# Two-layer attention kernel: loads, rotary products, second norm and first scores of the opening group in another order, and the layer-2 transposes of the chances ahead of the values

## Chip, cores and metric

One Trainium2 chip, one core. The metric is the device time of one execution in microseconds (us); three executions of the kernel before took 964.74, 966.09 and 969.46 us, median 966.09. The profile comes from a further execution. Engines are called as in the profile: PE (matrix), PEld (its weight loads), DVE (vector), ACT (scalar), POOL (GpSimd) and SP, which here only issues DMAs.

## What is computed

`x` is 8 batches of 512 tokens of 256 values, all in f32. Two layers:

```
xn = layernorm(x)
x  = x + causal_attention(xn) + int8_linear(xn)        # 16 heads of 64, rotary q and k, biases
xn = layernorm(x)
comparison = (xn @ left) @ (xn @ right).T / sqrt(256)
x  = x + ((comparison > threshold) * softmax(comparison + bias)) @ xn
       + sigmoid(xr @ Wr.T) * (relu(xk @ Wk.T)**2 @ Wv.T)   # xr, xk: mixes of xn and xn one token before
```

The int8 linear quantises `xn` with one scale for all batches, so the greatest absolute value of every batch is gathered while layer 1 runs (`amax`).

## The kernel before

**Order.** The order of the work is written out by hand, and each engine takes its instructions in that order, one queue per engine. What an instruction waits for stops everything behind it on its engine. DMAs are issued by SP, a few by ACT. The built program hands eight completion counters to the DMAs in turn, and a DMA is not issued before the earlier one on its counter has landed.

**Layer 1** runs over 16 groups `at`, two per batch, each of eight heads (four tiles of two heads). The steps of a group:

- `project_qk(p, which)` (L371): the product `pq` (L382, eight matmuls) for one half of a group's q (`which` 0) or k (1), then ACT evicts it with its bias into `l` (L387), and SP copies `l` into `y` with each pair of 32-row blocks exchanged (L389, four DMAs). `l` and `y` have two buffers for each name.
- `turn_qk` (L392): the rotary step. DVE makes `h = l*cos` and `y = y*sin` (L397), POOL adds them (L400). The result `h` is a head tile for the scores; the DMAs of a later `y` wait for this add when they use its buffer.
- `project_v` (L403) with the store of `va` (L418), and `load_v` (L423), which reads it back in another layout as `vr` (four DMAs, L428).
- `scores(at, run)` (L437): products `sc` (L448) for one of five runs of query blocks. `soften` (L455): DVE adds the mask and finds the maximum (L474), ACT makes the exponentials (L478). `divide` (L484): reciprocal on DVE (L489), scaling on POOL (L494). `turn` (L502): DVE transposes the chances (L514). `weigh` (L519): products `av` (L527) of a whole group; it needs all five runs turned.
- `look_at` and `prepare` (L285, L289): statistics and norm of the next batch's `x` on DVE (L151 to L161), with one small POOL step (L155), and `amax` (L293). `transpose_x` (L297): PE transposes it (L303), ACT copies it to `xnT` (L306), SP stores it (L307). The tile of `x` has one buffer.
- `load_rest` and `load_second` (L266, L133): five loads that ACT issues; `wo` is 1 MB.

All products take PSUM banks from one ring of eight, so a product also waits for the reader of the bank eight allocations before.

**The opening** (L714 to L746) is written out apart: batch 0's norm, projections (0,0) to (3,0), the values, and runs 0 and 1 of group 0. The other three runs of group 0 are in the loop at `at == 0` (L783 to L829), with the transposes of batch 1 between runs 2 and 3. The loads of the second half of the weights (`load_group(which, 2, 2)`, L725) and of batch 1 (L722) are issued inside the opening.

**Layer 2** (L901 to L948) runs over batches: `compare` (L595), `key` (L628), `turn_input` for the next batch (L216), `gate` (L642), `sides_of` (L228), `value` (L656), `turn_chances` (L668: PE transposes `trc`, ACT and DVE copy them in turn), `complete` (int8 part) and `end` (products `po`, L687, and output).

Of the kernel before, what the change touches and what calls it, by code (L numbers as in the profile page):

```python
# [8 lines left out]
F32 = mybir.dt.float32  # L9
# [3 lines left out]
ALU = mybir.AluOpType  # L13
# [31 lines left out]
def two_layers(  # L45
# [30 lines left out]
    def load_x(b, parts=1):  # L76
        t = xpool.tile([P, NT, D], F32, tag="x", name=f"x_{b}")
        for h in range(parts):
            rows = slice(h * NT // parts, (h + 1) * NT // parts)
            nc.sync.dma_start(t[:, rows, :], tokens(b)[:, rows, :])  # L80
        return t
# [4 lines left out]
    def load_group(which, g, n=1):  # L86
        nc.sync.dma_start(wqkv[which][:, g : g + n], (Wq, Wk, Wv)[which][:, g : g + n])
# [160 lines left out]
    with ExitStack() as c0:  # L248
# [37 lines left out]
            xt = x_next.pop(0)  # L286
            seen[b] = xt, statistics(xt, f"a{b}", parts=2 if b == 0 else 1)

        def prepare(b):  # L289
            xt, stats = seen.pop(b)  # L290
            normalise(xt, xt, stats)
            normed[b] = xt
            nc.vector.tensor_reduce(  # L293
                amax[:, b : b + 1], xt, AX.XY, ALU.max, apply_absolute_value=True
            )

        def transpose_x(b):  # L297
            xn = normed.pop(b)
            xnT[b] = whole(f"xnT_{b}")
            for k in range(NK):  # L300
                pb = bank(f"pxt_{b}_{k}")
                for t in range(NT):
                    nc.tensor.transpose(  # L303
                        pb[:, bass.ts(t, P)], xn[:, t, bass.ts(k, P)], ident
                    )
                nc.scalar.copy(xnT[b][:, k, :], pb)  # L306
            nc.sync.dma_start(xn_far[b], xnT[b].rearrange("p k n -> p (k n)"))  # L307


        spread = {}  # L310
# [80 lines left out]

        def turn_qk(at, which):  # L392

            l, y = evicted.pop((at, which))
            h = qk.tile([P, 2, S], F32, tag=f"h{which}", name=f"h_{at}_{which}")
            for dst, src, table in ((h, l, cs[:, :S]), (y, y, cs[:, S : 2 * S])):
                nc.vector.tensor_tensor(  # L397
                    dst, src, table[:, None, :].to_broadcast([P, 2, S]), ALU.mult
                )
            nc.gpsimd.tensor_tensor(h, h, y, ALU.add)  # L400
            heads_of[at, which] = h

        def project_v(at):  # L403
            b, g = divmod(at, NH)
# [309 lines left out]
        look_at(0)  # L714
        prepare(0)
        transpose_x(0)
        project_qk(0, 0)
        project_qk(0, 1)
        turn_qk(0, 0)
        project_qk(1, 0)  # L720
        turn_qk(0, 1)
        x_next.append(load_x(1))  # L722
        project_qk(1, 1)
        for which in (1, 0, 2):
            load_group(which, 2, 2)  # L725
        turn_qk(1, 0)
        project_v(0)
        turn_qk(1, 1)
        look_at(1)
        prepare(1)  # L730
        project_qk(2, 1)
        project_qk(2, 0)
        scores(0, 0)
        soften(0, 0)
        turn_qk(2, 1)
        divide(0, 0)
        project_qk(3, 1)
        load_v(0)
        load_rest()
        load_second()  # L740
        turn_qk(2, 0)
        project_qk(3, 0)
        scores(0, 1)
        soften(0, 1)
        turn(0, 0)
        divide(0, 1)  # L746
        for at in range(last):
            b, g = divmod(at, NH)
            two = at + 2 <= last
            if at >= 1:  # L750
                if g == 0 and b < B - 1:
                    fetch(b)
                if at in (last - 3, last - 2):
                    s_ = at - last + 3
                    fetch_output(s_, output_tile(f"x1e_{s_}"))
                    xnl = fetch_input(s_, work.tile([P, NK, S], F32, tag="xnl", name=f"xnl_{s_}"))
                scores(at, 0)
                turn(at - 1, 4)
                soften(at, 0)
                if at == last - 3:  # L760
                    scale_of_x()
                weigh(at - 1)
                keep_weighed(at - 1)
                turn_qk(2 * at + 2, 1)
                load_v(at)
                divide(at, 0)
                turn_qk(2 * at + 3, 1)
                if at == last - 2:
                    first_norm = norm(0, xpool.tile([P, NT, D], F32, tag="x", name="yn_0"))
                scores(at, 1)  # L770
                soften(at, 1)
                turn(at, 0)
            if g == 1 and b + 2 < B:
                look_at(b + 2)
            if at >= 1:
                divide(at, 1)
                project(at + 1, 0)
            elif at == 0:
                project_v(1)
            if at in (last - 3, last - 2):  # L780
                xq = work.tile([P, NK, S], BF16, tag="xq", name=f"xq_{s_}")
                quantise(s_, xnl, xq)
            if at == 0:  # L783
                turn_qk(3, 1)
            scores(at, 2)
            soften(at, 2)
            if at >= 1:
                turn_qk(2 * at + 2, 0)
            turn(at, 1)
            divide(at, 2)  # L790
            if g == 1 and b + 2 < B:
                prepare(b + 2)
            if at == last - 1:
                turn_qk(2 * at + 3, 0)
            if at >= 1:
                project_v(at + 1)
            else:
                transpose_x(1)
                x_next.append(load_x(2))
            if at == last - 1:  # L800
                break
            scores(at, 3)
            soften(at, 3)
            turn_qk(2 * at + 3, 0)
            turn(at, 2)
            divide(at, 3)
            if g == 0 and 1 <= b < B - 1:
                transpose_x(b + 1)
                if b + 2 < B:
                    x_next.append(load_x(b + 2))  # L810
            if at in (last - 3, last - 2):
                for half in range(2):
                    add_quantised(s_, half, xq, line(f"u_{s_}_{half}"))
            if 1 <= at < last - 1:
                finish(at - 1)
            if at == last - 2:
                first_norm()
            scores(at, 4)
            soften(at, 4)
            turn(at, 3)  # L820
            if two:
                project(at + 2, 1)
            divide(at, 4)
            if at == 0:
                spread_rest()
                spread_second()
                fetch(0)
            if g == 0 and b < B - 1:
                add_biases(b)  # L829
            if at == last - 4:  # L830
                greatest()
# [69 lines left out]
        for b in range(B):  # L901
            if b == 0:
                cut(prob, [P, 2, 4 * pitch(1) + 1, Q], "t1", 2)
                cut(prob, [P, 2, 4 * pitch(2) + 1, Q], "t2", 1)
                cut(work, [P, NP, D], "wo", 2)
            if b + 3 < B:
                fetch_late(b + 3)
            if b > 0:
                compare(b)
                kk = key(b)  # L910
            if b + 1 < B:
                turn_input(b + 1, whole(f"yt_{b + 1}", S + 1))
            if b > 0 and b + 2 < B:
                xq = clip_late(b + 2)
            if b == 0:
                pt = turn_chances(b)
            elif b + 1 < B:
                mix_before(b + 1, 1)
                mix_own(b + 1, 1)
            if b > 0:  # L920
                r = gate(b)
            if b + 1 < B:
                sides_of(
                    b + 1, *(attp.tile([P, S], F32, tag="att", name=f"lr_{b + 1}_{n}") for n in range(2))
                )
            if b == 0:
                mix_before(1, 1)
                mix_own(1, 1)
            if b + 1 < B:
                mix_before(b + 1, 0)  # L930
            if b > 0:
                for half in range(2):
                    value(b, half, r, kk)
            if b + 3 < B:
                round_late(b + 3)
            if b > 0:
                pt = turn_chances(b)
            if b + 2 < B:
                complete(b + 2, xq)
            if b + 1 < B:  # L940
                mix_own(b + 1, 0)
            y = work.tile([P, NT, D], F32, tag="v", name=f"y_{b}", bufs=2)
            end(b, (0,), pt, r, y)
            if b + 2 < B:
                normal = norm(b + 2, by_tokens(cuts["t0"][(b + 2) % 3]))
            end(b, (2,), pt, r, y)
            if b + 2 < B:
                normal()  # L948
# [66 lines left out]
```

## Time and profile before

| | |
|---|---|
| profiled execution | 965.37 us; span in the trace 963.6 us |
| busy share of the span | PE 97%, DVE 81%, POOL 58%, ACT 55% |
| mean granted PE clock | 0.993 |
| first score product of group 0 | starts at 42.54 us |
| `weigh` of group 0 | starts at 82.15, ends at 91.75 us |
| last product | ends at 959.95 us |

The page gives busy shares of the engines, the span in 40 slices, the chain of work that ended last, and groups of instructions. A row of a timeline reads: start, duration, engine, line, operation, output from input, count, and in brackets the idle time of the engine before it with what ended it. A row of the waits reads: who waited for what, us in total, times, longest. A row of the windows reads: the stretch and its length, busy us of PE, PEld, DVE, ACT and POOL with instruction counts, the granted PE clock, the DMA share and GB/s.

### The profile page before, as it was taken

The numbers are of one execution on the slowest core, as the hardware profiler recorded it, in microseconds if no ns is written. First come the engines' busy times: TensorE is split into PE (matmuls) and PEld (weight loads), VectorE is DVE, ScalarE is ACT, GpSimd is POOL, SyncE is SP. The second block draws the span as 40 slices with busy tenths as digits, with TensorE's granted clock in tenths as the row PEclk, the third lists the DMA queues.
The fourth block names the chain that finished last, engine by engine and source line by source line (L and its number), as shares of the span: only waits on it lengthen the run. The fifth ranks groups of instructions, "written<-read, shape, count | busy, mean of one in ns | idle before, by whom it ended". The sixth has DMA issues, their size and how long they took to land.

```text
span 963.6 us, 27433 instructions
## 1 busy us (share of the span) xinstructions
PE 935.6 (97%) x10491; PEld 596.7 (62%) x10491; DVE 784.7 (81%) x2429; ACT 529.8 (55%) x1480; POOL 561.3 (58%) x698
## 2 busy tenths in 40 slices
PE   9898999999999999999999998999998999999998
PEld 5345565656565565757565655665655677777776
DVE  4598988797889879978997897787899478888864
ACT  3364565555565656474756655554667335555553
POOL 3396766665655657566666664989766424444321
PEclk9999999999999999999999999999999999999999
DMA  6784345425453544254544435353444112221110
GB/s 183 210 244 103 97 111 153 102 77 139 145 116 83 136 136 128 73 133 116 127 108 133 115 88 155 111 155 89 94 118 123 45 59 71 70 77 55 34 33 33
DMA packets 60930, 105.40 MB, mean 109 GB/s; under 512 B 7552, under 2 KB 38272, under 8 KB 60800
## 3 DMA queue, kind: packets, MB, share of 16 engines
q1 hardware_dynamic: 58928, 102.01, 39.2%
q8 instruction: 83, 1.36, 0.7%
q10 hardware_dynamic: 1872, 1.64, 0.6%
q14 instruction: 47, 0.39, 0.1%
HBM read 39.14 MB, written 28.84 MB: 71 GB/s over the span
## 4 chain that ended last, share of the span: by engine, by line
PE 90%; DVE 4%; issue 2%; POOL 1%; DMA 1%; ACT 1%; SPq 1%; DVEq 0%; ACTq 0%; POOLq 0%
PE pq L382 21%; PE av L527 13%; PE sc L448 13%; PE pw L346 11%; PE pv L411 10%; PE po L687 5%; PE pg L649 3%; PE pvv L661 3%; PE pk L634 3%; PE plr L233 2%; PE trc L674 1%; PE c L606 1%; DVE y L397 1%; DVE p L474 1%; DVE t L514 1%
## 5 line engine op out<-in xcount | busy, mean ns | idle before, releaser
L478 ACT ACTIVATE p<-p,nm 128x64 f32<-128x64 f32 (+15 forms) x512 | 260.0, 511 | 151.6 <-DVE nm L474 122.0
L494 POOL TENSOR_SCALAR p<-p,rs 128x64 f32<-128x64 f32 (+15 forms) x512 | 268.4, 546 | 51.0 <-DVE rs L489 48.7
L400 POOL TENSOR_TENSOR h<-h,y 128x1024 f32<-128x1024 f32 x64 | 167.7, 2621 | 185.4 <-DVE y L397 97.3
L474 DVE CUSTOM_DVE_ANT_0 p<-sc,cmask 128x64 f32<-128x64 f32 (+15 forms) x512 | 191.1, 436 | 80.9 <-PE sc L448 78.9
L514 DVE STREAM_TRANSPOSE t<-p 128x256 f32<-128x256 f32 (+3 forms) x640 | 192.6, 366 | 18.6 <-POOL p L494 18.5
L448 PE MATMUL sc<-h,h 64*32 64x512 f32 (+15 forms) x4096 | 146.0, 397 | 7.6 <-issue 5.9
L527 PE MATMUL av<-t,vr 32*64 32x96 f32 (+15 forms) x4096 | 129.9, 397 | 7.2 <-issue 7.2
L448 PEld LDWEIGHTS sc<-h,h 64*32 64x32 f32 x4096 | 76.5, 106 | 94.6 <-issue 70.5
L527 PEld LDWEIGHTS av<-t,vr 32*64 32x64 f32 x4096 | 122.2, 132 | 14.3 <-issue 10.4
L382 PE MATMUL pq<-xnT,wk 128*128 128x512 f32 x256 | 116.1, 606 | 5.8 <-DMA wk<-in_Wk 4.3
L387 ACT ACTIVATE l<-pq,cs 128x512 f32<-128x512 f32 x128 | 84.3, 682 | 67.6 <-PE pq L382 57.8
L397 DVE TENSOR_TENSOR y<-y,cs 128x1024 f32<-128x1024 f32 x64 | 109.0, 1704 | 8.9 <-DMA y<-l 6.5
L382 PE MATMUL pq<-xnT,wq 128*128 128x512 f32 x256 | 114.4, 598 | 0.2 <-ACT xnT L306 0.2
L346 PE MATMUL pw<-wo,att 128*128 128x256 f32 x512 | 114.3, 381 | 0.0
L411 PE MATMUL pv<-wv,xnT 128*128 128x512 f32 x256 | 114.0, 598 | 0.0
L346 PEld LDWEIGHTS pw<-wo,att 128*128 128x128 f32 x512 | 95.9, 190 | 16.1 <-issue 3.7
L478 ACT ACTIVATION_READ_ACCUMULATOR p<-p,nm 128x1 f32 x512 | 97.0, 189 | 0.0
L382 PEld LDWEIGHTS pq<-xnT,wk 128*128 128x128 f32 x256 | 47.9, 192 | 67.2 <-issue 62.6
L411 PEld LDWEIGHTS pv<-wv,xnT 128*128 128x128 f32 x256 | 47.4, 190 | 57.7 <-issue 54.2
L382 PEld LDWEIGHTS pq<-xnT,wq 128*128 128x128 f32 x256 | 47.4, 190 | 56.6 <-issue 48.1
L397 DVE TENSOR_TENSOR h<-l,cs 128x1024 f32<-128x1024 f32 x64 | 78.4, 1225 | 4.3 <-ACT l L387 4.3
L541 ACT ACTIVATE att<-av,cs 128x512 f32<-128x512 f32 x64 | 38.9, 688 | 72.5 <-PE av L527 72.4
(111 smaller groups left out, 954.8 us busy)
## 6 DMA issues: line engine op xcount, KB each, us to landing
y<-l SPq DMA_DIRECT2D x256, 128.0 KB, 2.3
va<-v SPq DMA_DIRECT2D x32, 512.0 KB, 3.0
vr<-va SPq DMA_DIRECT2D x64, 256.0 KB, 4.6
x<-in_x SPq DMA_DIRECT2D x15, 512.0 KB, 4.2
xnf<-xnT SPq DMA_DIRECT2D x8, 512.0 KB, 3.4
x1f<-x SPq DMA_DIRECT2D x7, 512.0 KB, 3.4
out<-y SPq DMA_DIRECT2D x14, 256.0 KB, 2.2
cut_wo<-xnf SPq DMA_DIRECT2D x5, 512.0 KB, 3.8
```

Source lines behind the costliest of these rows:

```text
L346: nc.tensor.matmul(pw[:, j, :], atts[at, p][:, tok], wo[:, 4 * (at % NH) + p, :], start=(p == 0), stop=(p == 3),)
L382: nc.tensor.matmul(pb, w[:, g, k, bass.ts(t, P)], xnT[b][:, k, :], start=(k == 0), stop=(k == NK - 1),)
L387: nc.scalar.activation(l[:, t, :], pb, AF.Identity, bias=cs[:, bias : bias + 1])
L397: nc.vector.tensor_tensor(dst, src, table[:, None, :].to_broadcast([P, 2, S]), ALU.mult)
L400: nc.gpsimd.tensor_tensor(h, h, y, ALU.add)
L411: nc.tensor.matmul(pb.rearrange("p (g n) -> p g n", g=2), xnT[b][:, k, bass.ts(2 * half + j, P)], wqkv[2][:, 2 * g : 2 * g + 2, k, :], sta ...
L448: nc.tensor.matmul(scored[at, i][e][j * Q : j * Q + Q, :], q[rows, j % 2, bass.ts(i, Q)], k[rows, j % 2, :n], start=True, stop=True,)
L474: nc.vector.tensor_tensor_reduce(p[:, e, col : col + n], sc, cmask[:, S - n :], -1.0 / L**0.5, BIG, ALU.add, ALU.min, nm[:, c : c + 1],)
L478: nc.scalar.activation(p[:, e, col : col + n], p[:, e, col : col + n], AF.Exp, bias=nm[:, c : c + 1], scale=-1.0, accum_out=sm[:, c : c + 1],)
L494: nc.gpsimd.tensor_scalar(p, p, rs[:, c : c + 1], 1.0, ALU.mult, ALU.mult)
L514: nc.vector.transpose(turned[at][c][:, :, at_ : at_ + (n - 1) * pitch(c) + 1 : pitch(c), :], p[:, :, c * P : c * P + n * Q].rearrange("p e ...
L527: nc.tensor.matmul(banks[j][e * L : e * L + L, i * Q :], vs[at][rows, m, c, bass.ts(e, L)], t[c][rows, e, m * pitch(c) + m : m * pitch(c) ...
```

## The change

No product, copy or vector step is added or taken away. The order is changed in two places.

**Opening group.** Batch 1 is loaded straight after batch 0's transposes, and the store of batch 0's transposed input, which stood there, goes behind projection (2,1). The three loads of the second weight half are issued one by one: k behind projection (1,0), q behind (1,1), v behind (2,1). The rotary products are taken apart into `turn_own` (`l*cos`) and `turn_other` (`y*sin` and the add), and the statistics, norm and `amax` of batch 1 stand between them. Runs 0 and 1 of the scores come one after the other, ahead of projections (2,0), (3,1) and (3,0). The loop's special cases for `at == 0` are written out; there, `project_v(1)` comes behind run 2, `turn_qk(3, 0)` ahead of run 3, and the transposes of batch 1 behind the softening of run 3. The spreading of constants, the fetch of batch 0 and its bias add move from the end of group 0 into group 1.

**Layer 2.** For batches after the first, `turn_chances` comes ahead of `value`; for batch 0, the first mix of batch 1 comes ahead of `turn_chances`.

```diff
-        def prepare(b):
+        def prepare(b, *between):
             ...
             normalise(xt, xt, stats)
             normed[b] = xt
+            for f in between:
+                f()
             nc.vector.tensor_reduce(
                 amax[:, b : b + 1], xt, AX.XY, ALU.max, apply_absolute_value=True
             )
+        def keep_input(b):
+            nc.sync.dma_start(xn_far[b], xnT[b].rearrange("p k n -> p (k n)"))
...
+        def turn_own(at, which):
+            h = qk.tile([P, 2, S], F32, tag=f"h{which}", name=f"h_{at}_{which}")
+            times(h, evicted[at, which][0], 0)
+            heads_of[at, which] = h
+        def turn_other(at, which):
+            _, y = evicted.pop((at, which))
+            h = heads_of[at, which]
+            times(y, y, S)
             nc.gpsimd.tensor_tensor(h, h, y, ALU.add)
...
         transpose_x(0)
+        x_next.append(load_x(1))
         project_qk(0, 0)
+        turn_own(0, 0)
+        look_at(1)
+        turn_other(0, 0)
         project_qk(0, 1)
-        turn_qk(0, 0)
+        turn_own(0, 1)
         project_qk(1, 0)
-        turn_qk(0, 1)
-        x_next.append(load_x(1))
+        load_group(1, 2, 2)
+        def second_pair():
+            turn_other(0, 1)
+            turn_own(1, 0)
+        prepare(1, second_pair)
         project_qk(1, 1)
-        for which in (1, 0, 2):
-            load_group(which, 2, 2)
-        turn_qk(1, 0)
+        load_group(0, 2, 2)
+        turn_other(1, 0)
         project_v(0)
         turn_qk(1, 1)
-        look_at(1)
-        prepare(1)
         project_qk(2, 1)
-        project_qk(2, 0)
+        keep_input(0)
+        load_group(2, 2, 2)
         scores(0, 0)
         soften(0, 0)
+        scores(0, 1)
+        project_qk(2, 0)
         turn_qk(2, 1)
         divide(0, 0)
-        project_qk(3, 1)
+        soften(0, 1)
         load_v(0)
         load_rest()
         load_second()
+        project_qk(3, 1)
+        turn(0, 0)
         turn_qk(2, 0)
+        divide(0, 1)
         project_qk(3, 0)
-        scores(0, 1)
-        soften(0, 1)
-        turn(0, 0)
-        divide(0, 1)
+        turn_qk(3, 1)
+        scores(0, 2)
+        soften(0, 2)
+        turn(0, 1)
+        project_v(1)
+        divide(0, 2)
+        turn_qk(3, 0)
+        scores(0, 3)
+        soften(0, 3)
+        transpose_x(1)
+        x_next.append(load_x(2))
+        turn(0, 2)
+        divide(0, 3)
+        scores(0, 4)
+        soften(0, 4)
+        turn(0, 3)
+        project(2, 1)
+        divide(0, 4)
-        for at in range(last):
+        for at in range(1, last):
...
+            if at == 1:
+                spread_rest()
+                spread_second()
+                fetch(0)
+                add_biases(0)
...
+            if b + 1 < B:
+                mix_before(b + 1, 1)
+                mix_own(b + 1, 1)
             if b == 0:
                 pt = turn_chances(b)
-            elif b + 1 < B:
-                mix_before(b + 1, 1)
-                mix_own(b + 1, 1)
-            if b > 0:
+            else:
                 r = gate(b)
             if b + 1 < B:
                 sides_of(
                     ...
                 )
-            if b == 0:
-                mix_before(1, 1)
-                mix_own(1, 1)
+            if b > 0:
+                pt = turn_chances(b)
             if b + 1 < B:
                 mix_before(b + 1, 0)
             if b > 0:
                 for half in range(2):
                     value(b, half, r, kk)
...
-            if b > 0:
-                pt = turn_chances(b)
```

More of the change, by code (lines that the diff above doesn't have):

```diff
@@ L306, in transpose_x @@
                 nc.scalar.copy(xnT[b][:, k, :], pb)
-            nc.sync.dma_start(xn_far[b], xnT[b].rearrange("p k n -> p (k n)"))
+            if b > 0:
+                keep_input(b)
         spread = {}
@@ L392, in turn_qk, with times @@
         def turn_qk(at, which):
-            l, y = evicted.pop((at, which))
-            h = qk.tile([P, 2, S], F32, tag=f"h{which}", name=f"h_{at}_{which}")
[L396 to L399, printed above, removed]
+            turn_own(at, which)
+            turn_other(at, which)
+        def times(dst, src, first):
+            table = cs[:, first : first + S]
+            nc.vector.tensor_tensor(
+                dst, src, table[:, None, :].to_broadcast([P, 2, S]), ALU.mult
+            )
+        def turn_own(at, which):
+            h = qk.tile([P, 2, S], F32, tag=f"h{which}", name=f"h_{at}_{which}")
+            times(h, evicted[at, which][0], 0)
[4 more added lines that the diff above has]
+            times(y, y, S)
             nc.gpsimd.tensor_tensor(h, h, y, ALU.add)
-            heads_of[at, which] = h
         def project_v(at):
@@ L748, in two_layers @@
+        turn(0, 2)
[6 more added lines that the diff above has]
+        for at in range(1, last):
             b, g = divmod(at, NH)
             two = at + 2 <= last
[L750 to L772, printed above, removed]
+            if g == 0 and b < B - 1:
+                fetch(b)
+            if at in (last - 3, last - 2):
+                s_ = at - last + 3
+                fetch_output(s_, output_tile(f"x1e_{s_}"))
+                xnl = fetch_input(s_, work.tile([P, NK, S], F32, tag="xnl", name=f"xnl_{s_}"))
+            scores(at, 0)
+            turn(at - 1, 4)
+            soften(at, 0)
+            if at == last - 3:
+                scale_of_x()
+            weigh(at - 1)
+            keep_weighed(at - 1)
+            turn_qk(2 * at + 2, 1)
+            load_v(at)
+            divide(at, 0)
+            turn_qk(2 * at + 3, 1)
+            if at == last - 2:
+                first_norm = norm(0, xpool.tile([P, NT, D], F32, tag="x", name="yn_0"))
+            scores(at, 1)
+            soften(at, 1)
+            turn(at, 0)
+            if at == 1:
[3 more added lines that the diff above has]
+                add_biases(0)
@@ L773, in two_layers @@
             if g == 1 and b + 2 < B:
                 look_at(b + 2)
[L775 to L779, printed above, removed]
+            divide(at, 1)
+            project(at + 1, 0)
             if at in (last - 3, last - 2):
@@ L782, in two_layers @@
                 quantise(s_, xnl, xq)
-            if at == 0:
-                turn_qk(3, 1)
             scores(at, 2)
             soften(at, 2)
-            if at >= 1:
-                turn_qk(2 * at + 2, 0)
+            turn_qk(2 * at + 2, 0)
             turn(at, 1)
@@ L794, in two_layers @@
                 turn_qk(2 * at + 3, 0)
[L795 to L799, printed above, removed]
+            project_v(at + 1)
             if at == last - 1:
@@ L806, in two_layers @@
             divide(at, 3)
-            if g == 0 and 1 <= b < B - 1:
+            if g == 0 and b < B - 1:
                 transpose_x(b + 1)
@@ L813, in two_layers @@
                     add_quantised(s_, half, xq, line(f"u_{s_}_{half}"))
-            if 1 <= at < last - 1:
-                finish(at - 1)
+            finish(at - 1)
             if at == last - 2:
@@ L823, in two_layers @@
             divide(at, 4)
[L824 to L827, printed above, removed]
             if g == 0 and b < B - 1:
@@ L925, in two_layers @@
                 )
-            if b == 0:
-                mix_before(1, 1)
-                mix_own(1, 1)
+            if b > 0:
+                pt = turn_chances(b)
             if b + 1 < B:
```

## The prediction

> **What bounds the kernel now.** I read the page first. Its span slices show PE busy nearly throughout, so what counts is where PE stands still:
>
> ```profile
> PE   9898999999999999999999998999998999999998
> DVE  4598988797889879978997897787899478888864
> ```
>
> Next the waits of PE over the whole span, to see which of them the change can touch:
>
> ```profile
> PE av L527 <- issue: 7.2, 4, 4.2
> PE sc L448 <- issue: 5.9, 4, 2.5
> PE pq L382 <- DMA wk<-in_Wk: 4.3, 1, 4.3
> PE warm L103 <- POOL ident masks.py:199: 1.8, 1, 1.8
> PE pq L382 <- ACT xnT L306: 1.7, 2, 1.5
> PE pg L649 <- DVE e L622: 1.7, 1, 1.7
> PE sc L448 <- POOL h L400: 1.7, 2, 1.2
> ```
>
> By PE's timeline these fall as follows in the opening: 4.34 us at 29.47 to 33.81 (second weight half of k), 1.50 at 67.45 (`xnT` of batch 1), 0.46 at 76.04, 4.19 ahead of `weigh(0)` at 82.15. The 1.69 us of L649 is at 796.5, in layer 2's batch 1. All other waits lie in untouched stretches. Then the granted clock around the stalls, in the windows (fields: PE, PEld, DVE, ACT, POOL busy, PE clock, DMA share, GB/s):
>
> ```profile
> 34.00:38.00 4.00, 4.00 (x6) 1.60 (x6) 2.83 (x6) 0.69 (x1) 1.71 (x2) 0.57 0.93 326
> 66.00:68.00 2.00, 0.55 (x2) 0.31 (x3) 2.00 (x11) 1.88 (x8) 0.87 (x2) 1.00 0.67 232
> 82.00:86.00 4.00, 3.85 (x42) 3.38 (x50) 4.00 (x15) 2.94 (x9) 0.26 (x1) 0.57 0.67 154
> 594.00:598.00 4.00, 3.34 (x62) 1.60 (x62) 1.31 (x7) 0.58 (x2) 3.81 (x5) 0.57 0.69 157
> ```
>
> After the 4.3 us and 4.2 us stalls the clock is 0.57 for 4 us: the next eight `pq` take 5.37 us for 3.60, so such a stall costs 1.8 us more. The 1.5 us stall (second row) left it at 1.00. The fourth row follows a 2.55 us stall. So all that the change can take away is 4.34+1.77+1.50+0.46+4.19+1.8+1.69 = 15.75 us, 1.6%.
>
> **The opening up to the first scores.** SP issues the k weights at 28.90, behind a transfer that waits for a POOL add, and PE needs them at 29.47. In the new order they stand behind the (1,0) copies, which SP leaves at 24.43; with the old 4.77 us to landing they are there at 29.3. The stall and its slow clock (6.1 us) go. Batch 1's load goes at 8.8, where the store stood; statistics take 2.6 us and fit into DVE's idle 14.3 to 17.4.
>
> What is late next: only projection (2,1) (3.6 us) now stands between the values and `scores(0,0)`, where 8.8 us stood. PE is there at 33.05, and the last head of the pair comes from the add at 32.34 plus 2.34 = 34.7. The norm of batch 1 adds to this: its four L161 steps now fall on POOL's first add (19.7 to 22.1). The nearest row is the norm of another batch beside POOL's L494:
>
> ```profile
> 201.18 0.72 POOL L494 TENSOR_SCALAR p<-p,rs 128x384 f32<-128x384 f32 x1 [0.47 <-DVE rs L489]
> 201.37 0.68 DVE L161 TENSOR_SCALAR x<-x,mv_a,rstd_a 128x256 f32<-128x256 f32 x1
> ```
>
> The norm step ends 0.15 us after POOL's step and took 0.68, where 0.38 to 0.41 is usual with POOL idle. The Trainium skill (SBUF — State Buffer, section Who interferes with whom) says that a DVE instruction with at most one SBUF input and outside the two-port modes does not contend with GpSimd. The norm has one tensor input and costs 0.33 us for 256 elements, the pace per element of the two-input product (1.14 for 1024), so I read it as outside such a mode: by the rule the norm is free and the heads stay at 34.7. By the row it stands until the add ends. Then norm to 23.2, `y` (0,1) to 24.3, `h` (1,0) to 25.4, add to 27.8; the copies of (1,1) wait for that add (26.42 before), and everything behind is 1.45 us later: heads at 36.15. I take the row; zero and 1.7 are the ends.
>
> So PE stands at 33.6 to 36.15, 2.55 us. The skill (TensorE: Matmul & The Clock Gate, section Why this matters for your kernels) asks for no idle gap over about 3 us, by which this one is harmless. The fourth window row shows 0.57 after 2.55 us. I take the row: 1.7 us; by the rule 0.
>
> **From there to `xnT`.** PE: runs 0 and 1 about 3.5+1.7 to 41.35, (2,0) to 44.9. ACT evicts to 45.5, then does run 1's exponentials (3.94 us in the trace) to 49.45 and then only issues `load_rest`. Here SP's queue matters, by these two ACT issues:
>
> ```profile
> 48.17 0.43 ACTq L273 DMA_DIRECT2D wo<-in_Wo  x1
> 54.06 0.36 ACTq L135 DMA_DIRECT2D gs<-in_gates  x1
> ```
>
> The last of these waits in the built order for the counter of the first, so `wo` took 5.9 us. In the new order the third `vr` DMA of `load_v(0)` has that counter, and SP's copies of (3,1) stand behind it; before, they went ahead of `vr`. `wo` issued at 48.9 lands at 54.8; two `vr` issues (1.2) and four copies (2.4, the last landing 2.6 after its issue) bring `y` (3,1) to DVE at 60.4. Before:
>
> ```profile
> 61.10 1.21 DVE L397 TENSOR_TENSOR y<-y,cs 128x1024 f32<-128x1024 f32 x1
> 67.45 7.13 PE L382 MATMUL pq<-xnT,wk 128*128 128x512 f32 x16 [1.50 <-ACT xnT L306]
> 82.15 9.60 PE L527 MATMUL av<-t,vr 32*64 32x512 f32 x256 [4.19 <-issue]
> ```
>
> DVE thus enters run 2 only 0.7 us earlier. Behind it the new order is worse for PE. `xnT`'s copies came after run 2's exponentials (67.45 is 6.35 after 61.10). Now they come after run 3's, and run 3 on DVE stands behind `turn_qk(3,0)`: 1.14 (`y`) + 2.76 (soften) + 2.76 (turn) + 0.12 + 2.42 (rotary) + 0.55 (first of run 3) + 3.95 (exponentials) + 0.55 (copy) = 14.3. Projection (4,1) starts at 74.7, 7.3 us later than before, after more than 5 us in which PE has nothing left of group 0. It takes 7.13+1.8 to 83.6, `scores(1,0)` 1.95, `weigh(0)` 7.81: it ends at 93.35, against 91.75. DVE is done with the last turn near 81, so its 4.19 us wait is replaced by the `xnT` wait. **Sum of the opening: +1.6 us.**
>
> **Moved into group 1.** `spread` is 1.0 us of DVE and 0.7 of POOL; `add_biases(0)` 2.8 of POOL, ahead of `divide(1,1)`. Its fetch now stands behind `load_v(1)`, which waits for `weigh(0)`: landing about 6.5 after it, `divide(1,1)` from +10.3 to +15.0; its reader, DVE's turn at 107.36, is at +15.6. Hidden; DVE's 1.0 us lies in its 1.45 us idle at 102.17. If the cover is gone the next `weigh` (128.53, turned at 127.78) is late: 0 to 1 us; I take 0.
>
> **Layer 2.** For batch 0, mix and `mix_own` go ahead of DVE's copies, whose place they fill (DVE is idle 781.3 to 783.56). DVE reaches the next `compare` about 1.65 earlier, and the 1.69 us wait nearly goes: −1.5 (bounds −1.69 and +0.5, if `po` at 783.0 should wait for its copies). For later batches PE runs without a gap; `trc` moves 3.5 us ahead, but its input is complete 3.3 us before even that (898.6 against 901.9). Same work, no gap: 0. The tail has the same last product: 0.
>
> Total +1.6 −1.5 = +0.1 on the profiled 965.37, which lies 0.7 below the median of 966.09 (span 963.6 and 1.8 around it). On the median: 966.1 + 0.1 = **966.2 us**.
>
> **The rivals.** *Norm not held* (same class): heads at 34.7, gap too short for the clock, everything 3.1 us earlier at `y` (3,1): opening −1.5, total −3.0, 963.1. If held but no slow clock, 964.6. For it the skill's rule, against it the row; I count both inside the forecast.
>
> *The copies of (3,1) not held by `wo`*, 0.22. With the heads at 34.7 ACT ends the five issues and evictions near 50; copies from there land at 54.4, `weigh(0)` ends near 87.4 (−4.35); with `xnT` early enough for the clock to stay up, −6.15. With layer 2, −5.9 to −7.7: 959.3. For it: 1 MB could land quicker, as the 263 GB/s of the stretch 50 to 60 allows. Against: 5.9 us was measured beside lighter neighbours.
>
> *The loads jam SP*, slower, 0.14. The copies' third DMA shares its counter with `rw` (384 KB), behind `wo`. `wo`, `w8i`, `rw` and half of `vr` are 1.77 MB; at the 117 GB/s of 40 to 50 they take 15.1 us from 48.9, to 64.0. Then `y` is there at 67.2 and all is 6.8 later: 973.1. It decides once `rw` lands after about 62.
>
> **Chances.** Forecast with its variants 0.64, the fast rival 0.22, the slow one 0.14. About 0.5%, 4.8 us, is what a measurement of this kernel can tell from no change. Faster 0.22, same 0.63, slower 0.15. The likeliest case alone: 962.5 to 968. The range 959.3 to 970.5 reaches to the fast rival and part of the way to the slow one.
>
> **What the profile after would show.** Right: no PE wait for `wk`; first scores of runs 0 and 1 from 36; a pause at SP's third `vr` until `wo` lands, `y` (3,1) near 60; a PE wait of 5 us for `xnT` with clock 0.57 after; no L649 wait near 796. Wrong: norm steps of 0.4 us beside the add; `y` (3,1) before 57 or after 63; `xnT` copied before 70; a gap between `trc` and `pvv`.

## The result, and the profile after

The changed kernel takes 973.5 us (median of six runs, 972.02 to 974.62) where the kernel before takes 966.38 beside it: ratio 1.0071, interval 1.0054 to 1.0089. It is slower by 7 us. The forecast was 966.2, and its range ended at 970.5. The profiled execution took 973.5 us with a span of 971.7, which is 8.1 above the profiled execution of before; that one lay 1.0 below the median of its runs.

In the page's slices (24.3 us each), the third and fourth of PE fall from 9 and 8 to 7 and 7, and those of DVE from 9 and 8 to 5 and 7. The loss sits between 48.6 and 97 us.

```profile
PE   9877999999999999999999999999999999999998
DVE  6657897899889788977997898787989588888864
```

The waits of PE over the whole span (who waited for what, us in total, times, longest) show which stalls went and which came:

```profile
PE sc L467 <- DVE nm L493: 6.2, 1, 6.2
PE pq L388 <- ACT xnT L311: 6.0, 2, 5.7
PE sc L467 <- POOL h L420: 4.3, 2, 3.1
...
PE pg L668 <- DVE e L641: 1.1, 4, 0.4
```

The wait for the k weights is gone, as predicted. In its place stand 3.1 us for the head of (1,1), 6.2 us for run 3's banks, 5.7 us for `xnT`, and a new small wait in layer 2 that comes four times. PE's timeline puts them in order (start, duration, product, and in brackets the idle time ahead of it):

```profile
36.79 5.51 PE L467 MATMUL sc<-h,h 64*32 64x512 f32 x104 [3.06 <-POOL h L420]
...
67.99 3.82 PE L467 MATMUL sc<-h,h 64*32 64x320 f32 x64 [6.19 <-DVE nm L493]
...
79.62 9.93 PE L388 MATMUL pq<-xnT,wk 128*128 128x512 f32 x16 [5.71 <-ACT xnT L311]
...
91.37 8.01 PE L546 MATMUL av<-t,vr 32*64 32x512 f32 x256
```

`weigh` of group 0 ends at 99.38 instead of 91.75: the opening lost 7.6 us. DVE's timeline shows where. The four norm steps of batch 1 are the first row; the other two are the products `y*sin` of (2,0) and (3,1):

```profile
19.54 3.41 DVE L161 TENSOR_SCALAR x<-x,mv_a,rstd_a 128x256 f32<-128x256 f32 x4
...
55.94 1.22 DVE L405 TENSOR_TENSOR y<-y,cs 128x1024 f32<-128x1024 f32 x1 [4.66 <-DMA y<-l]
...
65.45 1.23 DVE L405 TENSOR_TENSOR y<-y,cs 128x1024 f32<-128x1024 f32 x1 [7.02 <-DMA y<-l]
```

DVE stands 4.66 and 7.02 us for the copies of `l` into `y`. The windows (PE, PEld, DVE, ACT, POOL busy, PE clock, DMA share, GB/s) show the DMA engines busy throughout in that stretch (share 1.06 and 1.11), and the clock low after each of PE's three long stalls:

```profile
37.00:41.00 4.00, 4.00 (x73) 1.91 (x61) 2.48 (x9) 1.99 (x5) 0.00 (x0) 0.57 1.05 332
...
54.00:58.00 4.00, 4.00 (x40) 1.95 (x25) 2.06 (x4) 2.31 (x4) 0.75 (x1) 1.00 1.06 242
58.00:62.00 4.00, 3.80 (x9) 1.33 (x7) 0.43 (x1) 0.00 (x0) 4.00 (x4) 1.00 1.11 228
...
66.00:70.00 4.00, 2.01 (x40) 1.71 (x48) 4.00 (x19) 2.75 (x11) 2.37 (x1) 0.50 0.01 4
...
78.00:82.00 4.00, 2.38 (x3) 1.17 (x4) 3.41 (x15) 3.15 (x12) 4.00 (x6) 0.56 0.29 105
```

SP's own waits in the opening, and then what the transfers issued between 46 and 66 us took from issue to landing (KB each, median us):

```profile
SPq L447 <- DMA wo<-in_Wo: 4.6, 1, 4.6
SPq L395 <- DMA vr<-va: 1.9, 1, 1.9
SPq L395 <- DMA rw<-in_rows: 0.8, 1, 0.8
```

```profile
y<-l SPq DMA_DIRECT2D x12, 128.0 KB, 4.4
...
vr<-va SPq DMA_DIRECT2D x4, 256.0 KB, 8.8
...
gs<-in_gates ACTq DMA_DIRECT2D x1, 3.0 KB, 7.7
```

SP waited for `wo` as predicted, and then also for the first `vr` and for `rw`. But over the whole kernel the copies and the pieces of `vr` land after 2.3 and 4.6 us; here they took about twice as long, and even the load of 3 KB took 7.7 us. The copies of (2,0) were issued at 46.7 to 49.2 with nothing holding SP, and DVE still got them only at 55.9. That is the main theory: **the copies share full DMA engines with `vr` (1 MB) and the five loads (1.6 MB)**. Its rivals: SP's wait at the counter alone; the norm held behind POOL's add; the late `xnT`; the order in layer 2.

### The profile page after: what moved, and what is told of

It is laid out like the page before. It is cut to its first block, busy times and chain, and to the rows that moved or that the text cites. A ratio compares the mean times of both kernels' runs of the same rounds, so it can differ in the third digit from the quotient of the medians.

```text
span 971.7 us, 27431 instructions
## 1 busy us (share of the span) xinstructions
PE 938.7 (97%) x10491; PEld 597.0 (61%) x10491; DVE 789.8 (81%) x2429; ACT 529.1 (54%) x1480; POOL 563.9 (58%) x698
## 4 chain that ended last, share of the span: by engine, by line
PE 80%; DVE 9%; DMA 3%; issue 3%; POOL 3%; ACT 1%; SPq 1%; DVEq 0%; ACTq 0%; POOLq 0%
PE pq L388 20%; PE av L546 13%; PE sc L467 13%; PE pw L352 10%; PE pv L430 9%; PE pg L668 3%; PE pvv L680 3%; PE po L706 2%; PE trc L693 1%; PE plr L233 1%; DVE mix L609 1%; DVE nm L629 1%; PE pk L653 1%; DMA y<-l 1%; DMA crl<-in_sides 1%
## 5 line engine op out<-in xcount | busy, mean ns | idle before, releaser
L467 PE MATMUL sc<-h,h 64*32 64x448 f32 (+15 forms) x4096 | 150.5, 405 | 17.0 <-issue 6.4
L467 PEld LDWEIGHTS sc<-h,h 64*32 64x32 f32 x4096 | 78.8, 108 | 104.8 <-issue 77.6
L388 PEld LDWEIGHTS pq<-xnT,wk 128*128 128x128 f32 x256 | 48.6, 194 | 67.8 <-issue 59.7
L430 PEld LDWEIGHTS pv<-wv,xnT 128*128 128x128 f32 x256 | 47.4, 190 | 57.8 <-issue 54.2
```

The costliest lines, as they stand in the source:

```text
L388: nc.tensor.matmul(pb, w[:, g, k, bass.ts(t, P)], xnT[b][:, k, :], start=(k == 0), stop=(k == NK - 1),)
L430: nc.tensor.matmul(pb.rearrange("p (g n) -> p g n", g=2), xnT[b][:, k, bass.ts(2 * half + j, P)], wqkv[2][:, 2 * g : 2 * g + 2, k, :], sta ...
L467: nc.tensor.matmul(scored[at, i][e][j * Q : j * Q + Q, :], q[rows, j % 2, bass.ts(i, Q)], k[rows, j % 2, :n], start=True, stop=True,)
```

## The experiments

A ratio is to the kernel before, run on the same chip beside it; where I give a difference in us between two kernels, it is the difference of their ratios times 966.4. From the two intervals such a difference is uncertain by 2 to 3 us, so those of e7, e8 and e14 lie at the edge of what can be told. Times and places ("`y` of (3,1) at") are of one profiled execution. In some of these the clock is low during the first scores and all behind them stands 1.3 to 1.6 us later: in the changed kernel, e5, e6, e12 and e14, but not in e1, e4, e7, e8, e11 and e13.

**e1: the new opening alone.** Layer 2's loop is put back to the order of before (the last two pieces of the diff undone).

> The new opening with layer 2 in the order of before. Theory A (the whole loss is the opening's: weigh of group 0 ends 7.6 us later, while layer 2's gain of 1.95 in batch 1 is given back at about 0.4 a batch): 973.2 us, within 0.5 of the changed kernel's 973.5. Rival (the forecast's own layer-2 term, -1.5, is right and the opening loses more than its 7.6): 975. In the profile: PE waits 1.7 us once for DVE's e in layer 2, and batches 2 to 6 are 24.6 us long, not 25.05.

973.2 us, ratio 1.0067 (1.005 to 1.0084). The loss is the opening's. Whether layer 2 gives the forecast's −1.5 is too close for this ratio; e2 measures it.

**e2: the new layer 2 alone**, with the opening of before.

> The opening of before with the new order of layer 2 alone. Theory A: batch 1 gains 1.95 us, each later batch loses about 0.4, together +0.3 on 966.4: 966.7. Rival (the losses of later batches come from the opening's changed phase and not from the order in layer 2): 964.5.

967.1 us beside 967.1, ratio 1.0002 (0.9992 to 1.0013). As theory A has it: no gain in total; −1.5 us would be a ratio of 0.9984. Its trace has batch 1 free of its wait and the later batches at 24.94 to 25.07 us, the same as in the changed kernel.

**e3: only the first mix ahead, in batch 0.**

```diff
-            if b == 0:
-                pt = turn_chances(b)
-            elif b + 1 < B:
+            if b + 1 < B:
                 mix_before(b + 1, 1)
                 mix_own(b + 1, 1)
+            if b == 0:
+                pt = turn_chances(b)
```

> The kernel before with one edit: in layer 2's batch 0 the first mix of batch 1 goes ahead of the chances; the later batches keep values ahead of chances. Theory A: the gain of batch 1 alone, -1.7 to -1.95: 964.5. Rival (the wait comes back in the next batch, since only DVE was moved): 966.4.

964.9 us beside 967.1, ratio 0.9985 (0.9974 to 0.9997): the gain is real (1.4 us by the ratio, 1.95 in the trace) and does not come back, since the batches after it stay at 24.6 us. So the part of the layer-2 change for batch 0 gains, and the part for the later batches gives it all back. How it does so is seen in DVE and POOL at batch 5. Before, with POOL's int8 add (L206) beginning 1.13 us after POOL's last step:

```profile
909.50 2.87 DVE L590 SCALAR_TENSOR_TENSOR mix<-yt,gs,mix 128x512 f32<-128x512 f32 x2
...
908.89 2.94 POOL L206 TENSOR_TENSOR x<-x,u 128x512 f32<-128x512 f32 x2 [1.13 <-DVE u L203]
```

After, with the comparison that follows:

```profile
917.13 3.39 DVE L609 SCALAR_TENSOR_TENSOR mix<-yt,gs,mix 128x512 f32<-128x512 f32 x2
...
917.02 2.95 POOL L206 TENSOR_TENSOR x<-x,u 128x512 f32<-128x512 f32 x2
...
929.42 0.92 PE L668 MATMUL pg<-wk,mix 128*128 128x256 f32 x3 [0.38 <-DVE e L641]
```

With the values behind the chances, POOL's gate adds end later, and L206 begins with DVE's mix instead of 0.6 us ahead of it. The mix takes 3.39 instead of 2.87 us, all that DVE does up to `e` is late, and PE waits. In before, `pg` had only 0.1 us to spare (the first of the four `e` starts at 895.86 and takes 0.74, to 896.60; `pg` starts at 896.70).

**e10: the mix ahead of that add** (new layer 2, opening of before).

```diff
-            if b + 2 < B:
-                complete(b + 2, xq)
             if b + 1 < B:
                 mix_own(b + 1, 0)
+            if b + 2 < B:
+                complete(b + 2, xq)
```

> The opening of before, layer 2 in the new order, with the second mix (the DVE steps of L609) put ahead of the int8 add, so that no mix step falls on POOL's L206. Theory (the mix takes 3.39 instead of 2.87 us beside that add, which the new order puts 0.57 later, and DVE is then 0.4 late at the next comparison): the wait for e at the gate (0.23 a batch in the trace, 0.38 in the distance of the products) goes, batches 24.6 us long, and batch 1's 1.95 stays: 964.5. Rival (chances ahead of values cost by themselves): 966.5.

963.9 us beside 965.2, ratio 0.9987 (0.9976 to 0.9997). The wait for `e` of 0.2 to 0.4 us is gone from the view, but the batches take 24.81 us, not 24.6, and `pg` starts 1.00 us after the start of the products ahead of it (`pyt`), where the distance is 0.88 in before. The mix now runs beside POOL's second gate add and takes 2.41 us, where 1.40 is usual. The theory is right in what it says of L206 and incomplete in its sum; that the slower mix makes the rest is likely, but no run takes it away.

**e4: loads and `vr` late.** The changed kernel, with the loads behind run 2's softening and `vr` behind projection (3,0).

```diff
-        load_v(0)
-        load_rest()
-        load_second()
         project_qk(3, 1)
...
         project_qk(3, 0)
+        load_v(0)
         turn_qk(3, 1)
         scores(0, 2)
         soften(0, 2)
+        load_rest()
+        load_second()
```

> The changed kernel with the five loads that ACT issues moved behind run 2's softening, and the reading back of vr moved behind projection (3,0), so that the copies of (2,0) and (3,1) meet no 1 MB transfers. Theory A (the transfers hold up the copies): the product y*sin of (2,0) near 51.5 and that of (3,1) at 55 to 58 instead of 55.9 and 65.45, PE's 6.2 us wait for run 3's banks goes, the wait for xnT stays near 5: 6 to 8 us off, 966. Rival N (the norm held behind POOL's add, with the slow clock at 37 to 41, sets the rest): 972. Rival X (run 3 ahead of xnT sets it by itself): y early, but weigh of group 0 not over 2 us earlier, 971.5.

963.9 us beside 967.1, ratio 0.9974 (0.9961 to 0.9988), 9.4 us better than the changed kernel and better than theory A expected. DVE's two products:

```profile
50.81 1.23 DVE L405 TENSOR_TENSOR y<-y,cs 128x1024 f32<-128x1024 f32 x1 [0.23 <-DMA y<-l]
...
54.52 2.07 DVE L405 TENSOR_TENSOR y<-y,cs 128x1024 f32<-128x1024 f32 x1 [1.22 <-DMA y<-l]
```

The copies land after 2.4 us again instead of 4.4:

```profile
y<-l SPq DMA_DIRECT2D x12, 128.0 KB, 2.4
```

The products come 5.1 and 10.9 us earlier (1.6 of each is the clock, which was full here at the first scores), the 6.2 us stall is gone, and `weigh` of group 0 starts at 80.32 instead of 91.37. The wait for `xnT`, which I expected to stay, shrank to 1.25 us after 3.76 us ahead of the transposes.

**e5 and e6: each alone.** e5 moves only the loads, e6 only `vr`, as in the diff above.

> The changed kernel with only the five loads of ACT moved behind run 2's softening; vr is still read back ahead of the copies of (3,1). Theory A1 (the loads hold the third vr at their counter and fill the DMA engines): no wait of SP for wo, y*sin of (3,1) at 57 to 59 (54.5 with vr moved too, 65.45 in the changed kernel), 965 to 967 us. Rival A2 (vr's own 1 MB, 8.8 us to landing, is the jam): y*sin of (3,1) after 62, 970 or more.

> The changed kernel with only the reading back of vr moved behind projection (3,0); the five loads stay at 48 to 53 us. Theory A1 (the loads are the jam): one of the copies of (3,1) still waits for wo's counter and lands beside w8i and rw; y*sin of (3,1) after 60, 968 to 971 us. Rival A2 (vr is the jam): y*sin of (3,1) at 54.5 to 57, 964 to 966.

e5: 966.8 beside 966.6, ratio 1.0001 (0.9982 to 1.002), 6.8 us better than the changed kernel. e6: 968.6, ratio 1.0028 (1.0014 to 1.0042), 4.2 us better. The product of (3,1) in e5, then those of (2,0) and (3,1) in e6:

```profile
58.20 1.25 DVE L405 TENSOR_TENSOR y<-y,cs 128x1024 f32<-128x1024 f32 x1 [3.93 <-DMA y<-l]
```

```profile
57.77 1.22 DVE L405 TENSOR_TENSOR y<-y,cs 128x1024 f32<-128x1024 f32 x1 [6.20 <-DMA y<-l]
...
60.69 2.85 DVE L405 TENSOR_TENSOR y<-y,cs 128x1024 f32<-128x1024 f32 x1 [0.43 <-DMA y<-l]
```

Against 54.52 with both moved, `y` of (3,1) is 3.7 us later with `vr` alone, 6.2 with the loads alone and 10.9 with both. About 1.5 us of each is the clock of these executions, which leaves about 2, 5 and 9: the loads are the greater share, and together they cost more than the sum. In e6, SP waited only 0.7 us for `wo`, and yet the copies of (2,0), which were issued by 49.5, came at 57.8. Neither A1 nor A2 is the whole.

**e13: the same traffic, without the wait at the counter.** The five loads are issued in the order `crl`, `gs`, `w8i`, `rw`, `wo`, so that `wo` shares its counter with a copy of (3,0).

```diff
-        load_rest()
-        load_second()
+        load_second()
+        load_rest()
```

and within `load_rest`, `wo` is last.

> The changed kernel with the same five loads at the same place, but issued in the order crl, gs, w8i, rw, wo. In the built program wo then shares its counter with the first copy of (3,0) and not with the third vr, so that nothing ahead of the copies of (3,1) on SP waits for wo; the bytes in flight are the same. Theory C (the wait at the counter is what holds up the copies): y*sin of (3,1) near 60, as with vr moved away (60.7), and 968.5 us. Theory D (the DMA engines are full, whoever waits): y*sin of (3,1) at 63 to 65.5, 971.5 to 973.5 us.

974.4 us beside 964.7, ratio 1.0092 (1.0064 to 1.012): no better at all. DVE's product of (3,1), `wo` from issue to landing, and what the four copies of (3,1), issued at 52.3 to 55.3, took to land (shortest, median, longest of those that the trace has):

```profile
64.51 1.23 DVE L405 TENSOR_TENSOR y<-y,cs 128x1024 f32<-128x1024 f32 x1 [11.21 <-DMA y<-l]
```

```profile
wo<-in_Wo ACTq DMA_DIRECT2D x1, 1024.0 KB, 13.4
```

```profile
DMA to landing us min/median/max: 9.1/10.0/10.9
```

SP issued all four `vr` by 52.2 and the copies of (3,1) 6 us earlier than in the changed kernel, and they came within 1 us of the same time, 9 to 11 us after their issue. SP does wait 7.0 us for `wo`, but only ahead of the copies of (3,0). The wait that the prediction counted only postponed part of the traffic; without it, `vr` is in the engines sooner (9.6 us to landing). Theory D holds.

**e14: the loads earlier**, behind run 0's softening.

```diff
         soften(0, 0)
+        load_rest()
+        load_second()
         scores(0, 1)
```

> The changed kernel with the five loads issued earlier instead of later: by ACT behind run 0's exponentials, near 42, where the DMA engines are busy for 0.19 of the stretch 41 to 46. Theory A (the loads do harm only where they meet the copies): as with the loads moved behind run 2, y*sin of (3,1) at 57 to 59 and 966.8 us. Rival (1.6 MB from 42 on still meet the copies of (2,0), issued at 46.7, and what stands behind them): 969 to 971.

968.3 us beside 964.7, ratio 1.0041 (1.0024 to 1.0057): 2.9 us better than the changed kernel, not the 6.8 of e5. `wo` lands about 48.8 and its counter now belongs to the first copy of (2,0), which SP holds for that; `y` of (3,1) comes at 60.6. The time lies between the two. The loads do fill the empty stretch (DMA share 0.76 in 41 to 46). The copies of (2,0), ready at about 46.7, leave SP only from 48.8, when `wo` is there, and then land after 2.2 to 2.3 us; those of (3,1) follow at 53.4, behind `vr`, where e5 has them at 51.8. Here the wait at the counter itself costs about 2 us: the 1.6 MB still meet the copies, as the rival says, but by a counter and not by full engines.

**e7: the norm off POOL's first add.** Norm and `amax` go behind the products of (1,1).

```diff
-        prepare(1, second_pair)
+        second_pair()
         project_qk(1, 1)
...
         turn_qk(1, 1)
+        prepare(1)
         project_qk(2, 1)
```

> The changed kernel with the norm of batch 1 and its amax moved from between the rotary products to behind those of (1,1), so that no norm step falls on POOL's first add; all loads stay. Theory A (the jam is the loss, the norm a part of it): heads at 34.7 instead of 36.73, no slow clock after the pause, the loads 2 to 3.5 us earlier and the jam with them: 970 to 971.5 us. Rival N (the held norm is the loss): 966. Rival Z (DVE gives it back, since norm and amax, 2.5 us, now stand ahead of run 0's softening): 973.5.

971.1 us beside 966.6, ratio 1.0043 (1.0021 to 1.0065), 2.7 us better. PE waits 1.07 us for the head instead of 3.06, everything up to `y` of (3,1), at 61.6, is about 4 us earlier (2.0 the wait, 1.6 the clock), and the stalls of 5.5 and 5.6 us behind it stay. The norm is not free of POOL here either: it falls on POOL's last add (32.65 to 35.10) and takes 3.41 us again, but no head waits for it there. The held norm is a part of the loss, not its core.

**e8: `xnT` ahead of run 3.**

```diff
         turn_qk(3, 0)
+        transpose_x(1)
+        x_next.append(load_x(2))
         scores(0, 3)
         soften(0, 3)
-        transpose_x(1)
-        x_next.append(load_x(2))
```

> The changed kernel with the transposes of batch 1 moved from behind run 3's softening to ahead of run 3's scores. The jam stays. Theory A+X (the jam sets when DVE enters run 2, and the late xnT adds the second wait): y*sin of (3,1) stays near 65.4, the 5.7 us wait for xnT goes, and weigh of group 0 is then set by DVE's last turn near 86.6: 4 to 5 us off, 969. Rival (the wait for xnT only moves into weigh, since DVE is what is late): 972 to 973.5.

971.4 us beside 966.6, ratio 1.0047 (1.0032 to 1.0062): 2.3 us better, half of what was expected. The wait for `xnT` goes, but 3.5 us of it return ahead of `weigh`, which then runs at the low clock (11.0 us instead of 8.0).

**e9: only the k weights early**, in the kernel before.

```diff
+        load_group(1, 2, 2)
         x_next.append(load_x(1))
         project_qk(1, 1)
-        for which in (1, 0, 2):
+        for which in (0, 2):
             load_group(which, 2, 2)
```

> The kernel before with one edit: the second weight half of k is loaded ahead of projection (1,1) and of batch 1's load, nothing else moves. Theory A (the early load alone takes the stall of 4.3 to 6.2 us and its slow clock; the other moves of the opening are what lost time): first scores near 36.7 instead of 42.5, PE and the copies behind it earlier by the same, 5 to 6 us off: 961. Rival (the stretch behind is bound by transfers, so that the stall comes back as a wait for the copies or as a longer wait ahead of weigh): 964.5 or more.

963.3 us beside 965.2, ratio 0.9974 (0.996 to 0.9988): 2.5 us, not 5 to 6. The stall moves to the next weights:

```profile
37.09 5.37 PE L382 MATMUL pq<-xnT,wq 128*128 128x512 f32 x8 [3.83 <-DMA wq<-in_Wq]
```

The changed kernel escapes this second stall, since it puts the scores of runs 0 and 1 ahead of the q weights' first use.

**e11 and e12: together.** e11 is the changed kernel with the edits of e7, e4 and e3 (for layer 2, only the first mix ahead). e12 adds that of e8.

> The changed kernel with three edits: norm of batch 1 behind the products of (1,1), ACT's five loads and vr late as before, and in layer 2 only batch 0's mix ahead. Theory A (the three losses are separate and add): 963.9 of the late loads, less 2.4 for the norm, less 2.2 for layer 2: 959.3. Rival (the norm's gain is lost again, because with heads at 34.7 DVE does norm and amax ahead of run 0): 961.7.

> The kernel of the run ahead of this one, with the transposes of batch 1 ahead of run 3's scores besides. Theory X (the 3.8 us in which PE waited ahead of the transposes, the 1.3 us for xnT and the slow clock after them go, and weigh of group 0 then waits for the last turn): 3 to 3.7 us less, 956. Rival (ACT copies xnT ahead of run 3's exponentials and makes DVE and POOL of runs 3 and 4 late by the 1.1 us of the copies, the wait moves into weigh): 958.5 to 959.5.

e11: 959.2 us beside 965.2, ratio 0.9931 (0.9914 to 0.9949). The sum of theory A is met: the three losses are separate and add. e12: 958.8, ratio 0.9927 (0.9911 to 0.9942); its step cannot be told from nothing. The rival's time is met, but its reason is not shown: in e12's profiled execution the wait ahead of `weigh` is only 1.06 us, and PE waits 2.56 us for the head where e11 waits 0.75, since DVE gets the copies of (1,1) at 32.52 instead of 30.62. The order of e11 and e12 is the same up to there, so this is a spread between executions. Both beat the kernel before: the new opening was worth having, once the transfers were taken out of its way.

## Why the prediction was wrong

**The stall for the k weights goes, and heads at 36.15:** right. The stall is gone; the first norm step was held until POOL's add ended at 21.83, the other three took 0.40 each:

```profile
18.57 3.26 POOL L420 TENSOR_TENSOR h<-h,y 128x1024 f32<-128x1024 f32 x1 [1.57 <-DVE y L405]
...
19.54 2.44 DVE L161 TENSOR_SCALAR x<-x,mv_a,rstd_a 128x256 f32<-128x256 f32 x1
```

The norm ended at 22.95 (23.2 predicted) and the heads came at 36.73. PE stood 3.06 us where 2.55 was reckoned, and the clock cost 1.6 (5.51 less the 3.91 us that the same products take in e4), where 1.7 was. That the clock fell was luck for the prediction: the last section shows that the length of the stall does not settle it. Taking the row, and not the rule of the Trainium skill (SBUF — State Buffer, section Who interferes with whom), was right here. The rule holds outside the two-port modes; whether the norm is outside them, as the prediction read from its pace, was not tried. e7 prices the norm at 2.7, against 3.1 in the rivals.

**"Two `vr` issues (1.2) and four copies (2.4, the last landing 2.6 after its issue) bring `y` (3,1) to DVE at 60.4":** this is the step that failed. Up to the landing of `wo` it held: 54.8 was predicted, and SP issued the third `vr` at 55.30. From there 5.6 us were reckoned, and it took 10.2, to 65.45. Two things were wrong in it. SP was to issue the copies at once, but it stood 1.9 us until the first `vr` had landed and 0.8 until `rw` had, both slow in the same traffic. And the last copy landed 4.66 us after its issue, not 2.6:

```profile
60.67 4.66 DMA y<-l
```

The 2.6 us are of a quiet stretch. The trace of before already had more for the copies of (3,1) and (3,0), issued at 52.2 to 60.7 beside and behind the same five loads (shortest, median, longest):

```profile
DMA to landing us min/median/max: 4.5/4.9/5.0
```

In the new order `vr` is in flight besides, 2.6 MB in all. e4 to e6 show that this traffic makes the loss at (3,1), and e13 that the wait for `wo`, on which the prediction built, does not decide it.

**The slow rival, 973.1,** had the bytes, but a chance of 0.14, and its time came close by luck. Its sum is wrong: half of `vr` is 0.52 MB, so that `wo`, `w8i`, `rw` and this are 2.03 MB and not 1.77, and at its 117 GB/s the total would be 975.4. It hung the delay on the counter of `rw`, where SP waited 0.8 us; the engines moved 228 to 305 GB/s in 50 to 62. `y` (3,1) came 1.75 us before its 67.2, and layer 2, which gained nothing instead of 1.5, took that back.

**From `y` (3,1) to projection (4,1), 14.3 us:** right, 14.17. The 6.19 us in which PE waited for run 3's banks was not foreseen, but adds nothing of its own, since `xnT` is set by DVE and ACT. Projection (4,1) took 9.93 where 8.93 was reckoned, since the clock stayed low longer; why is not shown (behind two stalls of like length the same products took 8.85 us in e7 and 9.09 in e13). The opening's 7.63 less the predicted 1.6 is 6.03: 4.92 from the start of this projection, 1.0 from its length, 0.1 behind it.

**Moved into group 1, 0:** right to 0.2 us; the loss is 7.63 at the end of `weigh(0)` and 7.81 at the first transposes of layer 2.

**Layer 2, −1.5:** wrong by 1.8, a smaller step that failed. Batch 1 gained 1.95 (1.5 predicted). "Same work, no gap: 0" for the later batches failed: PE ran without a gap, but with 0.1 us to spare, and the prediction asked only whether the inputs of `trc` were there, not what the later gate does to POOL's next step and so to DVE's mix. Four batches at 0.36 to 0.46 and 0.6 behind the last transposes give 2.3 back: the whole difference is 7.81 ahead of layer 2 and 8.14 at its last `po`.

Sum: +7.6, +0.2 and +0.3 make +8.1 on the profiled execution, where +0.1 was predicted.

## What to carry to other kernels

When an edit moves a load, add up the bytes in flight around every small transfer on the path, not only the waits of its queue: here small copies behind or beside 2.6 MB took twice as long and more, and another order of issue at the same place did not help (e13). An early load can merely move the stall to the next transfer, as in e9. Where the busiest engine has 0.1 us to spare, "same work, other order" is not free: ask which steps of DVE and POOL now run at the same time.

## What the hardware showed that was not expected

The low clock after a stall does not follow from its length. Of the eleven profiled executions of the new opening and its variants, a stall ahead of the first scores of 3.25 us (e8) left the 104 products at full pace, and one of 2.56 us (e12) did not:

```profile
37.14 3.92 PE L467 MATMUL sc<-h,h 64*32 64x512 f32 x104 [3.25 <-POOL h L420]
```

```profile
36.32 5.43 PE L467 MATMUL sc<-h,h 64*32 64x512 f32 x104 [2.56 <-POOL h L420]
```

Between them, 2.74, 2.84 and 2.90 us were followed by the full clock, and 2.77, 2.96, 3.06 and 3.07 by the low one; stalls of 0.75 and 1.07 us cost nothing. The rule that the prediction weighed, no gap over about 3 us (the Trainium skill, TensorE: Matmul & The Clock Gate, section Why this matters for your kernels), is therefore no threshold in this range, and neither is the single row that the prediction took. What decides was not tried. It makes 1.3 to 1.6 us of spread (5.24 to 5.51 us for the 104 products against 3.91) that an order of instructions does not explain.

The stall for the k weights in the opening of before differs between executions too: 4.34, 4.78, 6.09 and 6.15 us in four profiles of that same opening.
